# VectorE in program order in three stages of a sequence-mixing kernel, with the causal convolution's taps one pair behind its normalization

## The chip, the cores and the metric

The kernel runs on one core of one Trainium2 chip, in float32. The metric is the device time of one execution in microseconds (us). Engines are named as in the profile: PE is TensorE, DVE is VectorE, ACT is ScalarE, POOL is GpSimd and SP is SyncE, which issues most of the loads.

## What is computed

Two layers are applied one after the other to x of shape (4, 512, 128, 64): four batches, 512 time steps, and 128 frequencies of 64 channels, which together are D = 8192 columns. The change lies in the first layer, whose reference is this:

```python
xn = layernorm(x.reshape(b, t, d), ln_attn_g, ln_attn_b)
k = xn @ Wk
v = xn @ Wv
r = jax.nn.sigmoid(xn @ Wr)
decay = jnp.exp(-jnp.exp(w_decay))
# step: s = decay * s + kv_t, over time
attn = r * states @ Wo
x = x + attn.reshape(b, t, f, h)
xn = layernorm(x.reshape(b, t, d), ln_freq_g, ln_freq_b).reshape(b, t, f, h)
# convolution of 3 along the frequencies, over the 64 channels
fo = jax.nn.gelu(fo + freq_b[None, :, None])
x = x + fo
xn = layernorm(x.reshape(b, t, d), ln_time_g, ln_time_b)
# causal convolution of KS = 3 taps along time, each of the D columns by itself
to = to + time_b[None, :, None]
to = layernorm(jnp.swapaxes(to, 1, 2), time_ln_g, time_ln_b)
x = x + to.reshape(b, t, f, h)
mid = jax.nn.gelu(x @ ffn_W1 + ffn_b1)
x = x + (mid @ ffn_W2 + ffn_b2)
```

The second layer multiplies a few modes of a transform over time with learned weights, beside a moving average. It is not touched.

## The kernel before

Columns lie on the 128 partitions and the 512 time steps along the free axis. Two frequencies make a chunk of 128 columns, and two chunks make a pair, a tile of 128 by 2 by 512 (1024 elements on each partition). A batch has NPR = 32 pairs. A layernorm over all columns needs sums over the partitions and over all pairs; these are matmuls with a vector of ones (`add_up`, L249), followed by a short chain of small instructions (`finish`, `moments`, `rows`) that must end before the next stage can begin.

The first layer is cut into stages, each a Python generator that makes instructions for one pair and then yields:

- `project` (J): per pair a load of the weights, a load of x with columns on partitions, and a load of x with time on partitions ("token major"); the bn_stats of L338 on the latter (`statistics`), the scaling of the weights by the norm's gain on DVE (L355, `scale_weights`), and four matmuls of 512 columns (L407). For batch 0 there are also the matmuls of L396. For batches 2 and 3 the order of statistics and scaling is pinned and differs from that of batches 0 and 1.
- `scan` (Z): the recurrence over time, a chain of short instructions.
- `attend_and_convolve` (A): in round i, four pairs of matmuls give the attention of pair i (L527); DVE adds x (L531, into a tile `x1`, of which there are three) and scales by the rows of the norm (L535, `z`). Two rounds behind, the matmuls of the frequency convolution run (L553, L561, L569), ACT makes their gelu (L570), DVE adds `x1` (L576, `x2`), POOL stores `x2` (L577), ACT squares it (L578), and ACT scales two weight tiles for a later round (L546).
- `convolve_time` (C): per pair a load of `x2`, two DVE instructions of 1024 elements that normalize it (L625, L628, `normed`), then `tapped`: two ACT instructions that start `to` from the normalized tile (L633), four taps on DVE of 511 or 510 elements, two on each half of the tile (L637), a small correction and a store on POOL (L643, L644), and the square of `to` on ACT (L684). Its sums are added two steps behind.
- `open_feed` and `feed_forward` (O, F): residual, two matmuls with a gelu between, residual (L703 to L789).

`convolve_ahead` makes the first AHEAD = 14 pairs of the convolutions of batches 1 and 2 earlier, within the feed-forward of batches 0 and 1. For these batches `convolve_time` runs over the 18 remaining pairs, and fetches the 14 finished ones (`kh`) to square them (L691).

`in_turn` interleaves two sequences of stages. In each of eight pairs of stages it takes a step of one or of the other, according to their shares done and a lead. The pairs are:

```text
0: Z A of batch 0 | J Z of 1      4: O F of 1 | J Z of 3
1: C of 0 | A of 1                5: C of 2 | A of 3
2: O F of 0 | J Z of 2            6: O F of 2 | C O of 3
3: C of 1 | A of 2                7: F of 3 | nothing
```

The order in which instructions are made by the Python code is the program order. TensorE keeps it, by `tc.manual_schedule(engines={nc.tensor.engine})` around all of the above. For the other engines a planner chooses the order when the program is built, by its own costs; the result is a fixed sequence for each engine. Instructions given to `tc.keep_in_program_order` are exempt: they keep their place among each other. DVE, ACT and POOL each execute in the order so fixed, and wait on semaphores for what they read and for buffers to come free. The loads on SP's queue are in a fixed order as well.

Of the kernel before, what the change touches and what calls it, by code (L numbers as in the profile page):

```python
# [24 lines left out]
NPR = NCH // 2  # L25
# [55 lines left out]
def layer0(ctx, tc, dram, x, xt, vecs, wkvr, wo, wdec, wconv, fbias, w1, fb1, w2, fb2, x4):  # L81
# [4 lines left out]
    nc = tc.nc  # L86
# [18 lines left out]
    def two(pool, tag):  # L105
        return pool.tile([P, 2, SL], F32, tag=tag, name=tag)
# [183 lines left out]
    def load_x(b, i):  # L290
        xp = fr.tile([P, 2, SL], F32, tag="xp", name="xp")
        nc.sync.dma_start(xp, xt[b, 2 * i : 2 * i + 2].rearrange("c p t -> p c t"))
        return xp

    def spare(tag, n):
        return fr.tile([P, 2, n], F32, tag=tag, name=tag, bufs={"z": 4, "wx": 2}.get(tag, 3))
# [25 lines left out]
    def project(b):  # L322
        pa = two(ps_m, "m") if b == 1 else two(ps_a, "a")
        held[0] = b == 1
        if b == 0:
            psum_w = ps_p.tile([P, SL], F32, tag="p", name="psum_w")
        stt = rowp.tile([P, NT, NS, 6], F32, tag="stt", name="stt")
        def token_major(i, xk):
            s, h = i // 2, i % 2 * 2
            nc.sync.dma_start(  # L330
                xk, x[b, h * P : (h + 2) * P, s * SL : (s + 1) * SL].rearrange("(t p) d -> p t d", p=P)
            )
            return xk

        def statistics(i, xk):
            s, h = i // 2, i % 2 * 2
            for t in range(2):
                stats = nc.vector.bn_stats(stt[:, h + t, s, :], xk[:, t, :])  # L338
                if b > 1:

                    tc.keep_in_program_order(stats)

        def weights(i):

            if i < NPR:
                w = spare("wx", 4 * S + SL).rearrange("p k n -> p (k n)")[:, 0 : 16 * S]
                w = w.rearrange("p (c s) -> p c s", c=4)
                nc.sync.dma_start(w, wkvr[2 * i : 2 * i + 4, :, 0 : 4 * S].rearrange("c p s -> p c s"))
                for k in range(2):
                    ws[i + k] = w[:, 2 * k : 2 * k + 2, :]  # L350

        def scale_weights(i, wq, pinned=False):
            for j in range(2):
                w = wq[:, j, 0 : 3 * S]
                scaled = nc.vector.tensor_scalar_mul(w, w, vec[:, G1, 2 * i + j : 2 * i + j + 1])  # L355
                if pinned:
                    tc.keep_in_program_order(scaled)

        ws, xps, xks = {}, {}, {}
        if b > 1:  # L360
            weights(0)
            scale_weights(0, ws[0])
            xps[0] = load_x(b, 0)
        for i in range(NPR):
            first, last = i == 0, i == NPR - 1
            if b > 1:


                xks[i] = token_major(i, two(bk, "sq" if i % 2 else "x2"))
                if i % 2 == 0:  # L370
                    weights(i + 2)
                if not last:
                    xps[i + 1] = load_x(b, i + 1)
                wq, xp = ws.pop(i), xps.pop(i)
                for k in (i - 2, NPR - 2, NPR - 1) if last else (i - 2,):
                    if k in xks:
                        statistics(k, xks.pop(k))
            else:
                if unscanned[0]:

                    wq, xk = two(fr, "x1")[:, :, 0 : 4 * S + 3], spare("z", SL)
                else:

                    both = spare("wx", 4 * S + SL)
                    wq, xk = both[:, :, 0 : 4 * S], both[:, :, 4 * S :]
                n = 4 * S + 2 * (b == 0)
                nc.sync.dma_start(wq[:, :, 0 : n], wkvr[2 * i : 2 * i + 2, :, 0 : n].rearrange("c p s -> p c s"))
                xp = load_x(b, i)
                token_major(i, xk)
            if b == 0:  # L390
                nc.gpsimd.memset(wq[:, :, n:], 1.0)
                for j in range(2):
                    c = 2 * i + j

                    w = wq[:, j, :]
                    nc.tensor.matmul(  # L396
                        psum_w[0 : S + 2, 0 : 4 * S + 3], lhsT=w[:, 3 * S : 4 * S + 2], rhs=w,
                        start=c == 0, stop=c == NCH - 1,
                    )
            if b < 2:  # L400
                scale_weights(i, wq)
                statistics(i, xk)
            elif not last:
                scale_weights(i + 1, ws[i + 1], True)
            for j in range(2):
                for k in range(2):
                    nc.tensor.matmul(  # L407
                        pa[:, k, :], lhsT=wq[:, j, k * P : (k + 1) * P], rhs=xp[:, j, :],
                        start=first and j == 0, stop=last and j == 1,
                    )  # L410
                yield 1.0
        kvrg = rowp.tile([P, 2, SL], F32, tag="kvrg", name="kvrg")
        nc.scalar.copy(kvrg, pa)
        held[0] = False
        projected[b] = (kvrg, stt, psum_w) if b == 0 else (kvrg, stt)
# [242 lines left out]
    def convolve_time(b):  # L658
        bank = of_a if b == B - 1 else of_p
        made = AHEAD if b in ahead else 0  # L660
        moment = carried.pop(b)
        if made:
            rb, mb = ahead.pop(b)
        else:
            rb, mb = yield from rows(bank, *moment, "rm" if b == B - 1 else "rm3")
        st = bank()
        waiting, added = [], 0
        n = NPR - made
        for k in range(n + 2):
            while waiting and waiting[0][0] == k - 2:  # L670
                add_up(st, 0, *waiting.pop(0)[1:], added == 0, added == NPR - 1)
                added += 1
            if k < n:
                if b == B - 1:

                    x2, xr, to, sq = spare("xp", SL), spare("x1", SL), spare("z", SL), two(bk, "sq")
                else:
                    x2 = bk.tile([P, 2, SL], F32, tag="kx", name="x2", bufs=3)
                    xr, to = two(bk, "kd"), bk.tile([P, 2, SL], F32, tag="k3", name="to", bufs=3)
                    sq = bk.tile([P, 2, SL], F32, tag="sq4", name="sq4", bufs=2)  # L680

                normed(b, made + k, x2, xr, rb, mb, made > 0 and k < 4)
                tapped(b, made + k, xr, to)
                nc.scalar.activation(sq, to, AF.Square)  # L684
                waiting.append((k, to, sq))
                i = k * made // n
                if i != (k + 1) * made // n:

                    to = fetch("kh", tod, b, i)
                    sq = bk.tile([P, 2, SL], F32, tag="mid", name="sq5", bufs=4)  # L690
                    nc.scalar.activation(sq, to, AF.Square)  # L691
                    waiting.append((k, to, sq))
            yield 7.0 * (NPR + 2) / (n + 2)
        mean, sq = yield from finish(st, bank, 4)
        causal[b] = moments(mean, sq, 4)

# [137 lines left out]

    def in_turn(leads, *pairs):
        at, running = [0.0, 0.0], [None, None]

        def step(k):
            n = int(at[k])
            b, *stages = pairs[n][k]  # L840
            if running[k] is None:
                first = stages[0][0]
                if first in needed and b not in needed[first]:
                    return False
                running[k] = run(b, stages)
            share = next(running[k], None)
            if share == BLOCKED:
                return False
            if share is None:
                running[k] = None  # L850
                at[k] = n + 1.0
            else:
                at[k] = min(at[k] + share, n + 0.999)
            return True

        while min(at) < len(pairs):
            n = int(at[0])
            lead = leads[n] + (leads[n + 1] - leads[n]) * (at[0] - n) if n < len(pairs) else 0.0
            k = 1 if at[1] < at[0] + lead else 0
            if at[k] >= len(pairs) or not step(k):  # L860
                step(1 - k)

    def nothing(b):
        yield 1.0

    J, Z, A, C, O, F = project, scan, attend_and_convolve, convolve_time, open_feed, feed_forward
    begin[A] = 0
    needed = {A: scanned, C: carried, O: causal, F: opened}
    whole = {
        J: 2.0 * NPR, Z: 7 * CHAIN, A: 7.0 * NPR + 3 * CHAIN, C: 7.0 * (NPR + 2) + 3 * CHAIN, O: 4 * CHAIN,  # L870
# [338 lines left out]
```

## Time and profile before

| What | Value |
|---|---|
| Median of 3 runs | 3751.91 us (3749.89 to 3757.97) |
| The profiled execution | 3756.87 us |
| Its span, first to last instruction | 3755.1 us |
| Mean granted TensorE clock | 0.973 |
| TensorE busy | 3473.9 us, 93% of the span |
| DVE busy | 2675.7 us, 71% |
| ACT busy | 1778.4 us, 47% |
| POOL busy | 461.6 us, 12% |
| Moved by DMA | 910.58 MB, mean 242 GB/s |

The span runs from the first to the last instruction on the core. Busy time is the union of an engine's instructions, so two that overlap count once. A line such as L637 is a line of the kernel before. In the timeline a row gives the start, the duration from start to end, engine, line and operation, the output and the inputs with their shapes, and how many instructions are merged in it; a bracket at its end gives the time the engine stood idle before it and what it waited for. In a table of windows each row is a stretch of the span, with its length, the busy time of each engine (and instructions), the granted clock, and the share of the DMA engines that were busy.

### The profile page before, as it was taken

To read this page: it belongs to the slowest core of one execution; us is meant where nothing else is said; L and a number is where in the kernel's file an instruction comes from. 1 tells how busy PE (TensorE), PEld (TensorE's weight loads), DVE (VectorE), ACT (ScalarE), POOL (GpSimd) and SP (SyncE) were. 2 spreads that over 40 slices of the span, in tenths; PEclk is the share of its full clock that TensorE was granted. 3 is DMA by queue.
4 is the path that set the end of the run, shared out by engine and by line. 5 is a ranking of instruction groups with operands and counts; after the bars stand their busy time and mean duration, and the time that the engine had idled before them with its cause. 6 is when DMAs were issued, how large, how long until landed. Compare 5 with 4: busy or idle time off the path is not lost. (4 is left out here: it accounts for less than half of the span.)

```text
span 3755.1 us, 54524 instructions
## 1 busy us (share of the span) xinstructions
PE 3473.9 (93%) x20553; PEld 1381.1 (37%) x20553; DVE 2675.7 (71%) x3498; ACT 1778.4 (47%) x2331; POOL 461.6 (12%) x657
## 2 busy tenths in 40 slices
PE   8989988789998899999989989999988999899998
PEld 3433332224333223433322333343323843328533
DVE  4445659976767896676799699956658277792677
ACT  0013346645656564665656578868854200152100
POOL 0000013320110221011122122100000000001000
PEclk9999999999999999999999999999999999999999
DMA  9857647777885787788578577645569478894687
GB/s 309 275 197 250 227 150 265 257 265 260 291 277 169 244 285 264 269 296 273 182 252 287 202 247 267 229 157 185 201 197 283 151 240 292 287 292 165 215 284 261
DMA packets 427990, 910.58 MB, mean 242 GB/s; under 512 B 32976, under 2 KB 83920, under 8 KB 423632
## 3 DMA queue, kind: packets, MB, share of 16 engines
q1 hardware_dynamic: 354160, 637.18, 52.3%
q0 software_dynamic: 71680, 268.46, 19.9%
q8 instruction: 164, 2.69, 0.3%
q10 hardware_dynamic: 1888, 1.45, 0.1%
q14 instruction: 98, 0.80, 0.1%
HBM read 638.46 MB, written 268.50 MB: 242 GB/s over the span
## 5 line engine op out<-in xcount | busy, mean ns | idle before, releaser
L757 PE MATMUL p<-mid,w_sb 64*64 64x512 f32 x2048 | 554.1, 598 | 20.0 <-DVE wx L770 20.0
L757 PE MATMUL pb<-mid,w_sb 64*64 64x512 f32 x2048 | 535.3, 597 | 0.0
L749 ACT ACTIVATE mid<-c,fb_sb 128x1024 f32<-128x1024 f32 x256 | 284.6, 1112 | 98.7 <-PE c L744 96.5
L749 ACT ACTIVATE mid<-m,fb_sb 128x1024 f32<-128x1024 f32 x256 | 284.9, 1113 | 93.1 <-PE m L744 91.7
L744 PE MATMUL c<-x,w_sb 64*64 64x512 f32 x2016 | 281.5, 611 | 13.1 <-ACT ob L784 6.6
L744 PE MATMUL m<-x,w_sb 64*64 64x512 f32 x2016 | 282.9, 613 | 6.7 <-ACT ob L789 4.8
L757 PEld LDWEIGHTS p<-mid,w_sb 64*64 64x64 f32 x2048 | 155.5, 135 | 295.8 <-issue 262.6
L407 PE MATMUL a<-xp,wx 128*128 128x512 f32 x512 | 241.4, 615 | 9.1 <-DVE wx L355 8.6
L1055 ACT COPY two<-a 128x512 f32<-128x512 f32 x64 | 37.5, 586 | 432.9 <-PE a L1050 432.9
L1078 PE MATMUL b<-xin,avg_sb 128*128 128x512 f32 x512 | 230.8, 593 | 3.3 <-DVE xin L1084 3.3
L1084 DVE TENSOR_TENSOR xin<-b,pm 128x512 f32<-128x512 f32 x256 | 159.0, 683 | 102.9 <-PE b L1081 87.9
L527 PE MATMUL a<-rst,wo_sb 64*64 64x512 f32 x1024 | 147.8, 642 | 79.9 <-DVE x L531 78.3
L637 DVE SCALAR_TENSOR_TENSOR to<-kd,vec,to 128x510 f32<-128x510 f32 (+1 forms) x272 | 195.1, 743 | 4.2 <-issue 1.2
L712 ACT ACTIVATE kd<-kd,vec 128x512 f32<-128x512 f32 x256 | 192.9, 803 | 4.5 <-DVE kd L704 4.5
L937 DVE COPY xf<-b 128x256 f32<-128x256 f32 x128 | 54.3, 425 | 178.4 <-PE b L1024 177.4
L637 DVE SCALAR_TENSOR_TENSOR z<-x,vec,z 128x511 f32<-128x511 f32 x240 | 175.8, 744 | 5.7 <-ACT z L633 3.6
L715 DVE TENSOR_TENSOR x<-kd,kx 128x1024 f32<-128x1024 f32 x126 | 154.0, 1222 | 34.2 <-ACT kd L712 34.1
L531 DVE TENSOR_TENSOR x<-a,xp 128x1024 f32<-128x1024 f32 x128 | 156.1, 1219 | 23.0 <-PE a L527 19.3
L770 DVE SCALAR_TENSOR_TENSOR x4t<-p,fb_sb,x 128x512 f32<-128x512 f32 x64 | 47.9, 748 | 172.2 <-PE pb L757 169.8
L704 DVE TENSOR_TENSOR kd<-kd,rm 128x1024 f32<-128x1024 f32 x128 | 155.6, 1219 | 8.4 <-ACT rm L283 6.8
L703 DVE TENSOR_TENSOR kd<-kh,rm 128x1024 f32<-128x1024 f32 x128 | 155.6, 1219 | 6.0 <-ACT rm L283 3.2
L535 DVE TENSOR_TENSOR z<-x,rm 128x1024 f32<-128x1024 f32 x128 | 156.3, 1221 | 2.8
(276 smaller groups left out, 6743.2 us busy)
## 6 DMA issues: line engine op xcount, KB each, us to landing
xp<-in_xt SPq DMA_DIRECT2D x256, 512.0 KB
kh<-to SPq DMA_DIRECT2D x156, 512.0 KB
kx<-x SPq DMA_DIRECT2D x128, 512.0 KB
x<-ob POOLq DMA_DIRECT2D x64, 1024.0 KB, 8.4
xin<-x SPq DMA_DIRECT2D x64, 1024.0 KB
out<-xin POOLq DMA_DIRECT2D x64, 1024.0 KB, 6.3
x<-x POOLq DMA_DIRECT2D x98, 512.0 KB, 4.7
x<-x SPq DMA_DIRECT2D x96, 512.0 KB
```

The lines of the kernel that those rows point to most:

```text
L407: nc.tensor.matmul(pa[:, k, :], lhsT=wq[:, j, k * P : (k + 1) * P], rhs=xp[:, j, :], start=first and j == 0, stop=last and j == 1,)
L531: nc.vector.tensor_tensor(x1, at, xp, ALU.add)
L535: nc.vector.tensor_tensor(z, x1, pair_of(rb), ALU.mult)
L637: tap = nc.vector.scalar_tensor_tensor(to[:, j, k:], xr[:, j, : SL - k], vec[:, w, c], to[:, j, k:], ALU.mult, ALU.add)
L703: nc.vector.tensor_tensor(d, to, pair_of(rb), ALU.mult)
L704: nc.vector.tensor_tensor(d, d, pair_of(mb), ALU.subtract)
L712: tc.keep_in_program_order(nc.scalar.activation(d[:, j, :], d[:, j, :], AF.Identity, bias=vec[:, B4, c], scale=vec[:, G4, c]))
L744: nc.tensor.matmul(pm[halves[j], h, :], lhsT=w1_sb[halves[h], q * H : (q + 1) * H], rhs=x3[halves[h], j, :], start=True, stop=True,)
L749: nc.scalar.activation(mid, pm, AF.Gelu_apprx_tanh, bias=fb1_sb[:, q : q + 1])
L757: nc.tensor.matmul(sums2[i][j][halves[h], :], lhsT=w2_sb[halves[j], q, :], rhs=mid[halves[j], h, :], start=q == 0, stop=q == 3,)
L1078: nc.tensor.matmul(po[j], lhsT=avg_sb[:, j, :], rhs=xin[:, j, :], start=True, stop=False)
L1084: nc.vector.tensor_tensor(by_n(xin[:, j, :]), by_n(po[j]), by_c(pm[j % 2][:, j // 2, :]), ALU.add)
```

## The change

There are three edits.

1. In pairs 1, 3 and 5, those in which an `attend_and_convolve` runs beside a `convolve_time`, DVE too is put under `tc.manual_schedule`: its instructions keep the order in which the code makes them.
2. `convolve_time` normalizes pair k in step k (L625, L628) and taps pair k-1 in the same step (L633 to L644), with its square (L684) and that of any fetched `kh` (L691). There are n+3 steps instead of n+2, the sums are added three steps behind k, which is two behind the taps as before, and the weight that each step yields is adjusted.
3. `scale_weights` returns its last instruction, and in `project` for batches 0 and 1 the statistics are queued after it (`tc.issue_after`), so that L338 follows L355 of the same pair on DVE.

The built program has the same number of instructions on each engine as before: 10791 on PE, 3500 on DVE, 2347 on ACT, 662 on POOL and 1953 on SP. In the new kernel's file the lines lie a few further down: L531 becomes L532, L576 becomes L577, L637 becomes L638, and the squares of L684 and L691 move to about ten lines below.

```diff
@@ scale_weights
                 if pinned:
                     tc.keep_in_program_order(scaled)
+            return scaled.ins
@@ project
             if b < 2:
-                scale_weights(i, wq)
-                statistics(i, xk)
+                with tc.issue_after(scale_weights(i, wq)):
+                    statistics(i, xk)
@@ convolve_time
         n = NPR - made
-        for k in range(n + 2):
-            while waiting and waiting[0][0] == k - 2:
+        coming = None
+        for k in range(n + 3):
+            while waiting and waiting[0][0] == k - 3:
                 add_up(st, 0, *waiting.pop(0)[1:], added == 0, added == NPR - 1)
                 added += 1
+            tapping = coming
             if k < n:
 ...
                 normed(b, made + k, x2, xr, rb, mb, made > 0 and k < 4)
-                tapped(b, made + k, xr, to)
+                coming = xr, to, sq
+            if 0 < k <= n:
+                xr, to, sq = tapping
+                tapped(b, made + k - 1, xr, to)
                 nc.scalar.activation(sq, to, AF.Square)
-                waiting.append((k, to, sq))
-                i = k * made // n
-                if i != (k + 1) * made // n:
+                waiting.append((k - 1, to, sq))
+                for i in range((k - 1) * made // n, k * made // n):
 
                     to = fetch("kh", tod, b, i)
                     sq = bk.tile([P, 2, SL], F32, tag="mid", name="sq5", bufs=4)
                     nc.scalar.activation(sq, to, AF.Square)
-                    waiting.append((k, to, sq))
-            yield 7.0 * (NPR + 2) / (n + 2)
+                    waiting.append((k - 1, to, sq))
+            yield 7.0 * (NPR + 2) / (n + 3)
@@ in_turn
         at, running = [0.0, 0.0], [None, None]
+        region, ordered = ExitStack(), False
 ...
         while min(at) < len(pairs):
             n = int(at[0])
+            if ordered != (n in in_order):
+                ordered = not ordered
+                region.close()
+                if ordered:
+                    region.enter_context(tc.manual_schedule(engines={nc.vector.engine}))
             lead = leads[n] + (leads[n + 1] - leads[n]) * (at[0] - n) if n < len(pairs) else 0.0
             k = 1 if at[1] < at[0] + lead else 0
             if at[k] >= len(pairs) or not step(k):
                 step(1 - k)
+        region.close()
@@ the stages
     begin[A] = 0
+    in_order = (1, 3, 5)
```

## Prediction

> **What bounds the kernel now.** I read the page's head and slices first, then the windows by stage, then the timeline of VectorE (DVE) inside the stages that the change touches, and last the waits of the first stage.
>
> ```profile
> span 3755.1 us, 54524 instructions
> PE 3473.9 (93%) x20553; PEld 1381.1 (37%) x20553; DVE 2675.7 (71%) x3498; ACT 1778.4 (47%) x2331; POOL 461.6 (12%) x657
> DVE  4445659976767896676799699956658277792677
> ```
>
> Over the span TensorE is the full engine, but the DVE row has slices of 9, and these are the stages that the change puts in program order. Pair 1 (convolution of batch 0 beside attention of batch 1) runs from 545 to 803 us, pair 3 from 1242 to 1478, pair 5 from 1894 to 2140; the last two are cut where their convolution runs out.
>
> ```profile
> core 0: us, PE busy (x) PEld busy (x) DVE busy (x) ACT busy (x) POOL busy (x), PEclk, DMA share, GB/s
> 545.00:803.00 258.00, 214.85 (x1303) 64.21 (x1302) 254.47 (x278) 158.40 (x215) 81.47 (x93) 0.95 0.76 258
> 1242.00:1430.00 188.00, 169.62 (x1102) 49.43 (x1098) 181.84 (x185) 117.46 (x162) 42.87 (x61) 0.96 0.84 282
> 1430.00:1478.00 48.00, 45.95 (x298) 12.80 (x294) 22.87 (x20) 25.39 (x36) 7.25 (x10) 1.00 0.68 229
> 1894.00:2067.00 173.00, 152.97 (x990) 44.44 (x990) 169.23 (x174) 108.56 (x148) 42.66 (x57) 0.97 0.86 287
> 2067.00:2140.00 73.00, 68.01 (x441) 22.47 (x438) 46.44 (x47) 36.02 (x49) 12.01 (x17) 0.98 0.66 224
> ```
>
> In pair 1 DVE is busy 254.47 of 258 us: every DVE nanosecond added there is on the path. In pairs 3 and 5 it is full only while the convolution lasts; in the tails it is idle 25.1 and 26.6 us, and TensorE, at 45.95 of 48 and 68.01 of 73, sets the pace.
>
> What DVE pays for an instruction depends on its neighbour. In pair 1 the two stages alternate:
>
> ```profile
> 641.67 1.22 DVE L576 TENSOR_TENSOR both<-c,x 128x1024 f32<-128x1024 f32 x1
> 642.80 0.74 DVE L637 SCALAR_TENSOR_TENSOR to<-kd,vec,to 128x510 f32<-128x510 f32 x1
> 643.46 1.22 DVE L531 TENSOR_TENSOR x<-a,xp 128x1024 f32<-128x1024 f32 x1
> 644.60 0.74 DVE L637 SCALAR_TENSOR_TENSOR to<-kd,vec,to 128x511 f32<-128x511 f32 x1
> 645.26 1.21 DVE L535 TENSOR_TENSOR z<-x,rm 128x1024 f32<-128x1024 f32 x1
> ```
>
> From start to start a 1024-element instruction takes 1.13 us and a tap 0.66, less than the shown 1.22 and 0.74. In pair 3 the attention's three stand together:
>
> ```profile
> 1427.72 3.14 DVE L637 SCALAR_TENSOR_TENSOR to<-kd,vec,to 128x511 f32<-128x511 f32 x4
> 1430.97 1.22 DVE L576 TENSOR_TENSOR x<-m,x 128x1024 f32<-128x1024 f32 x1
> 1432.29 1.23 DVE L531 TENSOR_TENSOR x<-a,xp 128x1024 f32<-128x1024 f32 x1
> 1433.55 1.23 DVE L535 TENSOR_TENSOR z<-x,rm 128x1024 f32<-128x1024 f32 x1
> 1436.62 1.22 DVE L576 TENSOR_TENSOR x<-c,x 128x1024 f32<-128x1024 f32 x1 [1.85 <-ACT c L570]
> ```
>
> L576 to L531 is 1.32 us here (1.31 usually: L531 writes the x1 buffer, of three, that L576 has just read), and L531 to L535, which reads its x1, is 1.26 (1.25). The same way I read 0.779 for two taps on one half of a tile, and 1.245, once, from L625 to L628, which rewrites its output. So a dependent neighbour costs 0.175, 0.116, 0.118 and 0.11 us more.
>
> **What the Trainium skill says.** "Vector Engine (DVE) Microarchitecture Reference", section 5.2, gives 1.0417 ns a column and some 75 ns an instruction, by estimate 1.14 us for 1024; the trace agrees (1.134). "Perfetto Trace Analysis", "Optimizing Scalar/DVE Operations", says that the write-acknowledgement half of an instruction's overhead overlaps with the next; the trace agrees: 0.08 us of 1.22. "VectorE: DVE Perf Modes", "The DRAIN you can't avoid", says of eight copies that a semaphore after each costs nothing extra. Here a neighbour that waits costs 0.11 to 0.18 us; the measurement decides, but this feeds a rival.
>
> **The change part by part.** No instruction or DMA is added or removed (DVE has 3500 in both, counted in the built programs). All that changes is order, read from the built programs.
>
> *Pair 1.* Each round becomes L576, L531, L535, L625, L628 and four taps (two on one half, two on the other). Dependent neighbours rise: L576–L531 from 3 to 30, L531–L535 from 8 to 34, L625–L628 from 0 to 32, taps of one half from about 0 to 64; L637 to L625 on one kd slot falls from 7 to 3. Added: 27×0.175 = 4.7, 26×0.116 = 3.0, 32×0.11 = 3.5, 64×0.118 = 7.5, less 0.5: **+18.3 us**, 0.65 a round of 8.31. DVE is full, so nothing covers it. The edges: two L625 that now run before the first L576 follow it (+2.3); after the last L576 less is left (−3.4); the first weight scaling (L355) of the next projection now stands behind the attention's closing L266 to L275, where it used to stand ahead of that chain, and the first matmul of J2 waits some 2.4. Sum **+19.6**. Bounds +8 (L625–L628 and taps at nothing) to +24.
>
> *Pairs 3 and 5.* Eighteen convolution steps among 32 rounds. The built order puts about two behind every three attention rounds, and the last 3 rounds before the end without, against 5 before. A round with a step is 1.31 + 1.25 + 1.135 + 1.245 + 1.135 + 0.779 + 0.667 + 0.779 + 0.661 = 8.96 us. A round without is not the 3.70 of its DVE work: ScalarE, in its order, has the squares of the taps and of kh (L684, L691), that of L578, two scalings (L546) and the gelu (L570) that the next L576 needs, at pitches 0.95, 0.95, 0.95, 0.69 and 1.0; with the wait between, 4.84 from L576 to L576. Following the rounds from 1254.55 us (second L576; 1256.36 before), with TensorE's 5.65 to 7.4 us a round in the tail, the last L576 comes at 1477.2 against 1473.93: +3.3, and +2.3 for the weights behind the chain as above: **+5.6**. Pair 5 by the same count, where the next stage has no first matmul waiting longer: **+4.8**. Bounds −10 to +12 each: I multiply hand-read pitches over 30 rounds.
>
> *J0 and J1.* The statistics (L338) now follow the weight scaling. They wait on loads, and the scaling waited behind them on DVE:
>
> ```profile
> engine line waited for: us in total, times, longest us
> DVE stt L338 <- DMA z<-in_x: 53.8, 29, 8.8
> ...
> PEld a L407 <- DVE x L355: 24.6, 33, 5.5
> ...
> PE a L407 <- DVE x L355: 9.4, 7, 4.7
> ```
>
> What that can give is small, since loads are the pace: the window has a DMA share of 0.92 at 306 GB/s. TensorE needs 4.55 us for each of 31 intervals, 141.05; the weight loads are issued over 145.88; the excess is 4.8, and the first matmul comes 1.5 earlier: −6.3 at most. Against it, nine pairs' token-major loads of J1 that used to be issued early within J0 now fall into 164 to 232 us, where statistics stand ahead of the scan's short chains: +1 to +4. I take **−3** (−6.3 to +3).
>
> *Pair 6 and the rest* is not in program order; convolution of batch 3 only taps a step later, beside feed-forward work that keeps TensorE busy 269 of 300 us and hides it: 0 ± 3. The later add of statistics (L249) stands one step later in TensorE's order and costs only at a stage's end, where it is within the tails above.
>
> Sum: 19.6 + 5.6 + 4.8 − 3 + 0 = **+27.0 us**. The profiled execution took 3756.87 us, span 3755.1; it is 5 above the median of three, 3751.91, and nothing in the sum scales with that. **3779 us**.
>
> **Rivals.**
>
> *The tails close* (faster). With convolution spread to within three rounds of the end, pairs 3 and 5 could become as full as TensorE allows: busy 215.6 of 236 us and 221.0 of 246, so up to 20.4 + 25.0 = 45. At three quarters, −34 + 19.6 − 3 = −17: **3735**. It decides from 24 us recovered. For: the idle 25 us. Against: TensorE is already 96% busy in the 48 us tail, and a bare round is held at 4.84 by ScalarE.
>
> *The price is not paid.* If the 0.11 to 0.18 us come from something else than the neighbour, pair 1 keeps +1.3, pairs 3 and 5 lose some 4 each of their L625–L628 and taps, J gives −3: 1.3 + 1.6 + 0.8 − 3 = +0.7, **3753**. For: the skill's page. Against: the same lines show both pitches in one trace, by neighbour.
>
> *kh arrives late* (slower still). In pair 3 L691 waited on its load 26.5 us in 9 times, 53.0 over the run in 21, 2.5 each, behind slack. With DVE in program order a late square holds the gelu behind it, and L576 with all behind. A third of the 28 at 2.5 is 24: **3803**.
>
> That the order stays as it was is excluded by the built program.
>
> **How the numbers follow.** The sum of its parts (3765 to 3792, bounds not all at one end) 0.63; kh late 0.14; price not paid 0.10; tails close 0.13. Within 0.2%, 7.5 us, about what a measurement of this kernel can tell from no change, lies the second last and a little of the main case's fringe: 0.11. Faster 0.13, slower 0.76. The range 3748 to 3803 leaves out the closing tails and the upper part of kh late, 0.2.
>
> **What would show it.** Right: pair 1 about 277 us with as many DVE instructions; L576 to L531 at 1.31, L531 to L535 and L625 to L628 at 1.25, taps in fours of 2.96 us shown instead of twos of 1.40; the first L407 of J2 waiting on L355; rounds without a step at 4.84; J0 some 3 to 6 us shorter. Wrong: pair 1 at 258 with rounds of 8.3; DVE idle in the tails of pairs 3 and 5 much under 25 us; L691's waits well over 53 us and L576 waiting on L570 for as much.

## The result and the profile after

The changed kernel takes 3779.69 us (median of 6 runs, 3771.07 to 3789.77); the kernel before, run beside it, 3754.94 us. The ratio is 1.007, 95% interval 1.005 to 1.009: slower by 25 us. The profiled execution took 3788.66 us, 9 above the median of its kernel and 31.8 above the profiled execution of before, so the stages below show some 7 us more than the medians do.

The page's head and the DVE row of its slices, after:

```profile
span 3786.9 us, 54574 instructions
PE 3484.7 (92%) x20553; PEld 1382.8 (37%) x20553; DVE 2691.9 (71%) x3498; ACT 1783.6 (47%) x2331; POOL 435.5 (12%) x657
DVE  3445559976777886677789799956659267793677
```

DVE is busy 16.2 us longer with the same 3498 instructions. The windows after: pair 1, cut at the same places of the work as before, and pairs 3 and 5, each from the second L577 to the end of the convolution's last tap, and from there to the end of the last L577, which is the tail:

```profile
core 0: us, PE busy (x) PEld busy (x) DVE busy (x) ACT busy (x) POOL busy (x), PEclk, DMA share, GB/s
542.00:820.00 278.00, 219.99 (x1314) 62.23 (x1306) 267.82 (x278) 159.67 (x215) 64.30 (x91) 0.94 0.70 237
1270.40:1467.10 196.70, 174.61 (x1124) 50.48 (x1120) 181.19 (x181) 119.68 (x161) 41.44 (x60) 0.96 0.78 265
1467.10:1498.80 31.70, 30.43 (x202) 8.55 (x194) 14.70 (x13) 17.51 (x25) 4.46 (x7) 1.00 0.70 240
1934.20:2113.90 179.70, 157.13 (x1008) 45.12 (x1000) 170.27 (x172) 111.98 (x149) 39.42 (x57) 0.96 0.80 273
2113.90:2167.30 53.40, 51.34 (x335) 16.78 (x334) 37.62 (x36) 28.01 (x38) 7.93 (x12) 1.00 0.68 228
```

The same four stretches of pairs 3 and 5 before:

```profile
1256.40:1430.90 174.50, 159.08 (x1040) 46.22 (x1036) 168.57 (x171) 111.45 (x152) 39.72 (x56) 0.96 0.84 283
1430.90:1475.10 44.20, 42.94 (x284) 12.17 (x274) 22.00 (x18) 22.85 (x34) 5.84 (x9) 1.00 0.68 232
1908.20:2067.80 159.60, 142.44 (x932) 41.18 (x928) 156.78 (x162) 103.22 (x140) 39.75 (x53) 0.97 0.87 288
2067.80:2133.20 65.40, 63.26 (x418) 20.18 (x410) 45.02 (x42) 33.58 (x48) 9.43 (x14) 1.00 0.68 230
```

In pair 1 the same 278 DVE instructions are busy 267.82 us instead of 254.47. In pairs 3 and 5 the convolution lasts longer and the tails are shorter. In the tails DVE is idle 17.0 and 15.8 us, where it was 22.2 and 20.4; but up to the last tap it is now idle 15.5 and 9.4 us, where it was 5.9 and 2.8. The timeline of DVE in pair 1 shows a round. (Line numbers in a fence are those of the kernel that it shows. L633, L684 and L691 of before are L634, L690 and L696 in the changed kernel.)

```profile
644.35 1.22 DVE L577 TENSOR_TENSOR both<-c,x 128x1024 f32<-128x1024 f32 x1
645.66 1.23 DVE L532 TENSOR_TENSOR x<-a,xp 128x1024 f32<-128x1024 f32 x1
646.92 1.23 DVE L536 TENSOR_TENSOR z<-x,rm 128x1024 f32<-128x1024 f32 x1
648.06 1.22 DVE L626 TENSOR_TENSOR kd<-x,rm 128x1024 f32<-128x1024 f32 x1
649.32 1.23 DVE L629 TENSOR_TENSOR kd<-kd,rm 128x1024 f32<-128x1024 f32 x1
650.46 2.98 DVE L638 SCALAR_TENSOR_TENSOR to<-kd,vec,to 128x511 f32<-128x511 f32 x4
653.35 1.22 DVE L577 TENSOR_TENSOR x<-m,x 128x1024 f32<-128x1024 f32 x1
```

From L577 to L577 it is 9.00 us, with no idle time in any row: 1.31, 1.26, 1.14, 1.26, 1.14 and four taps of 2.89 together. All 24 rounds of pair 1 with one step take 9.0.

To say where time goes I cut every profiled execution at the same instructions: the first L531 of batch 1, the first L407 of batch 2, its last, the first L407 of batch 3, its last, the last L576 of batch 3, and the first matmul of the second layer. The kernels of the experiments are named below; times are us.

| Kernel | to pair 1 | pair 1 | pair 2 | pair 3 | pair 4 | pair 5 | 6 and 7 | second layer | span |
|---|---|---|---|---|---|---|---|---|---|
| before | 527.7 | 285.5 | 344.9 | 321.2 | 338.1 | 314.5 | 646.2 | 976.9 | 3755.1 |
| after | 524.5 | 307.7 | 346.4 | 326.8 | 339.5 | 321.2 | 649.0 | 971.8 | 3786.9 |
| e1 statistics alone | 526.3 | 286.9 | 346.5 | 322.3 | 340.1 | 318.3 | 646.3 | 969.4 | 3756.1 |
| e4 planner | 519.0 | 286.5 | 346.5 | 319.3 | 339.5 | 316.1 | 649.3 | 972.2 | 3748.4 |
| e2 pair 1 alone | 517.2 | 304.8 | 347.8 | 321.7 | 337.6 | 318.4 | 649.7 | 968.4 | 3765.7 |
| e3 pairs 3, 5 alone | 520.3 | 287.8 | 346.0 | 326.5 | 339.2 | 319.0 | 648.6 | 970.2 | 3757.6 |
| e5 taps in turn | 526.6 | 296.9 | 346.7 | 332.3 | 340.1 | 328.5 | 648.6 | 976.7 | 3796.5 |
| e6 interleaved | 520.5 | 286.3 | 346.9 | 337.6 | 341.5 | 330.3 | 648.9 | 970.3 | 3782.3 |
| e8 four x1 | 522.7 | 301.5 | 347.5 | 321.5 | 341.1 | 316.4 | 641.9 | 971.6 | 3764.3 |
| e7 no kh square | 518.9 | 306.3 | 347.9 | 314.6 | 341.2 | 318.3 | 650.4 | 971.7 | 3769.2 |
| e9 gelu ahead | 515.8 | 298.6 | 347.5 | 348.0 | 339.0 | 342.2 | 649.9 | 980.9 | 3821.9 |
| e10 planner, taps | 517.3 | 284.1 | 345.0 | 326.8 | 339.3 | 315.5 | 645.3 | 970.2 | 3743.5 |
| e11 and four x1 | 514.8 | 292.6 | 346.3 | 317.5 | 337.5 | 315.2 | 638.5 | 971.9 | 3734.3 |
| e12 joined | 518.4 | 285.2 | 347.5 | 319.8 | 339.3 | 315.2 | 639.9 | 974.3 | 3739.6 |

The first and the last stage show how far one execution can be trusted. After, e2 and e7 have the same order on DVE up to the end of pair 1 and still spread over 7.3 us before it; the second layer, which no edit touches, spreads over 12.5. The pairs between are steadier: pair 1 of after, e2 and e7, which share its code, is 307.7, 304.8 and 306.3. A profiled execution can lie up to 11 us from the median of its kernel (e10), so what a kernel takes as a whole is read from the ratios below, and the table only says where.

### The profile page after: what moved, and what is told of

Same layout as the page of the kernel before. It is cut to its first block, busy times and chain, and to the rows that moved or that the text cites. A ratio compares the mean times of both kernels' runs of the same rounds, so it can differ in the third digit from the quotient of the medians.

```text
span 3786.9 us, 54574 instructions
## 1 busy us (share of the span) xinstructions
PE 3484.7 (92%) x20553; PEld 1382.8 (37%) x20553; DVE 2691.9 (71%) x3498; ACT 1783.6 (47%) x2331; POOL 435.5 (12%) x657
## 5 line engine op out<-in xcount | busy, mean ns | idle before, releaser
L762 PE MATMUL p<-mid,w_sb 64*64 64x512 f32 x2048 | 562.7, 599 | 20.9 <-DVE wx L775 20.6
L749 PE MATMUL c<-x,w_sb 64*64 64x512 f32 x2016 | 286.3, 611 | 9.6 <-ACT mid L754 7.4
L528 PE MATMUL a<-rst,wo_sb 64*64 64x512 f32 x1024 | 155.7, 674 | 93.3 <-DVE x L532 91.7
L638 DVE SCALAR_TENSOR_TENSOR to<-kd,vec,to 128x511 f32<-128x511 f32 (+1 forms) x272 | 197.7, 748 | 4.8
L634 ACT ACTIVATE to<-kd,vec 128x512 f32<-128x512 f32 x136 | 103.5, 807 | 166.7 <-DVE kd L629 85.7
L532 DVE TENSOR_TENSOR x<-a,xp 128x1024 f32<-128x1024 f32 x128 | 156.7, 1224 | 34.1 <-PE a L528 25.6
L638 DVE SCALAR_TENSOR_TENSOR z<-x,vec,z 128x511 f32<-128x511 f32 x240 | 176.0, 746 | 5.6 <-ACT z L634 4.2
```

The costliest lines, as they stand in the source:

```text
L528: nc.tensor.matmul(at[hs, j, :], lhsT=wo_sb[halves[j], hs], rhs=rst[halves[j], :], start=True, stop=True)
L532: nc.vector.tensor_tensor(x1, at, xp, ALU.add)
L638: tap = nc.vector.scalar_tensor_tensor(to[:, j, k:], xr[:, j, : SL - k], vec[:, w, c], to[:, j, k:], ALU.mult, ALU.add)
L749: nc.tensor.matmul(pm[halves[j], h, :], lhsT=w1_sb[halves[h], q * H : (q + 1) * H], rhs=x3[halves[h], j, :], start=True, stop=True,)
L762: nc.tensor.matmul(sums2[i][j][halves[h], :], lhsT=w2_sb[halves[j], q, :], rhs=mid[halves[j], h, :], start=q == 0, stop=q == 3,)
```

## The experiments

Each ratio is to the kernel before, run on the same chip.

**e1, the third edit alone**, on the kernel before:

```diff
-                scale_weights(i, wq)
-                statistics(i, xk)
+                with tc.issue_after(scale_weights(i, wq)):
+                    statistics(i, xk)
```

> The kernel before with the third edit alone (in project for batches 0 and 1 the statistics follow the weight scaling on VectorE). Both theories: about 3 us faster than before, from a first projection that is some 10 us shorter (first to last L355) and a scan of batch 0 that gives most of it back. If the whole gain of the first projection stayed it would be 6 us; if nothing, 0.

3750.37 us, ratio 0.9993 (0.9982 to 1.0005): near the 3 us that were expected, but not told apart from no change. The first projection did get shorter: its last L407 started at 156.7 us instead of 163.5 (156.3 in the changed kernel).

**e4, the planner again**, on the changed kernel: `in_order = ()`.

> The changed kernel with in_order = (): the planner orders VectorE in pairs 1, 3 and 5 again, the second and third edit stay. Theory (neighbours: what costs is the 0.11 to 0.18 us that an instruction pays when its predecessor on VectorE produces or frees what it needs): the planner mixes the two stages, rounds of pair 1 are back at 8.3 us, and the whole is 20 to 28 us faster than the changed kernel, about 3752. Rival (shift: what costs is the tapping one step later, with its longer life of the kd tile and the later sums): pairs 1, 3 and 5 stay long, and the time stays near 3780.

3754.46 us, ratio 1.0002 (0.9991 to 1.0012). Pairs 1, 3 and 5 are back within 2 us of before. The shift of the taps by a step costs nothing that shows (the interval overlaps that of e1); the loss lies in program order.

**e2 and e3, program order in part**: `in_order = (1,)` and `in_order = (3, 5)`.

> The changed kernel with in_order = (1,): program order on VectorE in pair 1 alone, the planner in pairs 3 and 5. If the parts add up: from the first matmul of pair 1's attention to the first of the next projection some 21 us more than before, pairs 3 and 5 within 2 us of before, the whole 17 to 20 us slower than before, about 3772. If program order costs chiefly at the stages' edges or by what is drawn into them, pair 1 is nearer to before's.

> The changed kernel with in_order = (3, 5): the planner in pair 1, program order in pairs 3 and 5. If the parts add up: pair 1 as before within 2 us, pairs 3 and 5 some 6 us longer each, the whole 8 to 12 us slower than before, about 3763; this and the kernel with pair 1 alone together explain the changed kernel's loss.

e2: 3776.62 us, ratio 1.0052 (1.0035 to 1.007). e3: 3764.04 us, 1.0021 (1.0011 to 1.003). The parts add up: 0.52% and 0.21% make 0.73%, where the whole was 0.7%. In e2 pair 1 is 19.3 us longer than before, in e3 pairs 3 and 5 together 9.8. Both came out about as expected.

**e5, the taps in turn**, on the changed kernel, so that no tap follows the one whose result it adds to (ACT starts both halves before the first tap):

```diff
-        for j in range(2):
-            for k, w in ((1, W1), (2, W0)):
+        for k, w in ((1, W1), (2, W0)):
+            for j in range(2):
```

> The changed kernel, but the four taps of a pair go 511, 511, 510, 510 with the halves in turn, so that no tap follows the one it depends on; everything else in program order as it is. Theory (neighbours): two taps a round save 0.118 us each; pair 1 is 64 x 0.118 = 7.5 us shorter, rounds go from 9.00 to 8.77 us, pairs 3 and 5 win up to 36 x 0.118 = 4.2 us each, less what their tails hide; in all 8 to 16 us faster than the changed kernel, 3764 to 3772. Rival (fixed order: VectorE stands waiting for the one stage while the other has work ready): nothing changes, 3780.

Half of this came true. In pair 1 the rounds are 8.75 us, with 2.65 for the four taps instead of 2.89, and the pair is 296.9, 9.4 shorter than the mean of the three executions above (306.3; 7.5 expected). But pairs 3 and 5 became 5.5 and 7.3 longer than in the changed kernel, and the whole is 3789.01 us, ratio 1.0098 (1.0079 to 1.0117). Of the 15 rounds with one step in each, eight in pair 3 and six in pair 5 take 11.0 instead of 9.0. The timelines of DVE and of ACT in such a round of pair 3:

```profile
1356.26 2.73 DVE L640 SCALAR_TENSOR_TENSOR to<-kd,vec,to 128x511 f32<-128x511 f32 x4
1361.10 1.23 DVE L577 TENSOR_TENSOR x<-c,x 128x1024 f32<-128x1024 f32 x1 [2.12 <-ACT c L571]
```

```profile
1356.52 1.52 ACT L634 ACTIVATE to<-kd,vec 128x512 f32<-128x512 f32 x2 [1.83 <-DVE kd L629]
1359.10 1.06 ACT L705 ACTIVATE sq<-to 128x1024 f32<-128x1024 f32 x1 [1.06 <-DVE to L640]
1360.07 1.01 ACT L571 ACTIVATE c<-c 128x1024 f32<-128x1024 f32 x1
```

Here the planner put the square of the taps (L705) ahead of the gelu (L571) on ACT. In such a round of the changed kernel the gelu stands first: L571 starts at 1367.04 and the square, L690, at 1368.44. In e5 the square waits for the last tap, the gelu stands behind it, and DVE, whose order allows nothing else, waits 2.12 us for the gelu. DVE's waits on the gelu in pair 3 are 38.6 us in all, against 30.4 in the changed kernel and 23.8 before.

**e6, interleaved by hand**, on the changed kernel: the same three pairs in program order, but the code makes the convolution's DVE instructions between the attention's. `slots` holds two taps of the step; `fill()` makes the next one after L531 and after L576.

```diff
             nc.vector.tensor_tensor(x1, at, xp, ALU.add)
+            fill()
...
             nc.vector.tensor_tensor(x2, cv, x1s.pop(i), ALU.add)
+            fill()
...
+                one_tap(made + k - 1, xr, to, 1, 1)
+                slots.append(lambda k=k, xr=xr, to=to: one_tap(made + k - 1, xr, to, 0, 2))
+                slots.append(rest)
```

> The changed kernel, VectorE in program order in pairs 1, 3 and 5 as before, but the convolution's instructions are made between those of the attention: L576, tap, L531, tap, L535, L625, tap, L628, tap. No instruction follows the one it depends on. Theory (neighbours): rounds of pair 1 are 8.3 us instead of 9.0, pair 1 is 20 us shorter than in the changed kernel; pairs 3 and 5 win some 18 x 0.65 = 11 us less what the tails hide; in all 25 to 40 us faster than the changed kernel, 3740 to 3755. Rival (fixed order): the order is as fixed as it was, so pair 1 stays near 278 us and the whole near 3780.

Again half of it came true. DVE in pair 1:

```profile
660.08 1.22 DVE L634 TENSOR_TENSOR kd<-x,rm 128x1024 f32<-128x1024 f32 x1
661.22 0.74 DVE L666 SCALAR_TENSOR_TENSOR to<-kd,vec,to 128x511 f32<-128x511 f32 x1
661.88 1.22 DVE L639 TENSOR_TENSOR kd<-kd,rm 128x1024 f32<-128x1024 f32 x1
663.01 0.74 DVE L666 SCALAR_TENSOR_TENSOR to<-kd,vec,to 128x511 f32<-128x511 f32 x1
663.68 1.22 DVE L578 TENSOR_TENSOR x<-c,x 128x1024 f32<-128x1024 f32 x1
664.81 0.74 DVE L666 SCALAR_TENSOR_TENSOR to<-kd,vec,to 128x510 f32<-128x510 f32 x1
665.47 1.22 DVE L532 TENSOR_TENSOR x<-a,xp 128x1024 f32<-128x1024 f32 x1
666.60 0.74 DVE L666 SCALAR_TENSOR_TENSOR to<-kd,vec,to 128x510 f32<-128x510 f32 x1
667.26 1.22 DVE L537 TENSOR_TENSOR z<-x,rm 128x1024 f32<-128x1024 f32 x1
668.39 1.22 DVE L634 TENSOR_TENSOR kd<-x,rm 128x1024 f32<-128x1024 f32 x1
```

The nine instructions of a round take 8.31 us, the order as fixed as in the changed kernel, and pair 1 is 286.3, that of before. So the loss of pair 1 is the price of dependent neighbours and not of a fixed order. But pairs 3 and 5 are 10.8 and 9.1 us longer than in the changed kernel, and the whole is 3786.24, ratio 1.0089 (1.0071 to 1.0108). In pair 3, ACT and then DVE:

```profile
1369.77 1.52 ACT L660 ACTIVATE to<-kd,vec 128x512 f32<-128x512 f32 x2 [3.90 <-DVE kd L639]
1371.19 1.00 ACT L572 ACTIVATE m<-m 128x1024 f32<-128x1024 f32 x1
```

```profile
1372.22 1.22 DVE L578 TENSOR_TENSOR x<-m,x 128x1024 f32<-128x1024 f32 x1 [1.97 <-ACT m L572]
```

The start of the next taps (L660) waits for the normalization, the gelu waits behind it, and what stood between them on DVE in the changed kernel, four taps of 2.89 us, is here only one: 1.97 us idle. DVE's waits on the gelu in pair 3 are 51.8 us in all. This code also fetches the kh tiles later: their squares (L739) waited 14.4 us on the loads in pair 3, against 6.6 in the changed kernel, and no run says how much of the loss is due to that.

**e8, four x1 buffers** instead of three, on the changed kernel: `bufs=4` for the tag `x1`. L531 then writes a buffer that was read a round earlier.

> The changed kernel with four x1 buffers instead of three, all else the same: L531 (now L532) writes a buffer that was read a round earlier, and not the one that L576 ahead of it has just read. Theory (the 0.17 us from L576 to L531 are the wait for that buffer): the step from L576 to L531 falls from 1.31 to 1.14 us, rounds of pair 1 from 9.00 to 8.83, pair 1 is 26 x 0.17 = 4.4 us shorter; pairs 3 and 5 change by less than 3. Rival (it is the PSUM bank or the engine's drain that makes L531 late): 1.31 stays, and so does pair 1.

3768.0 us, ratio 1.0043 (1.0026 to 1.0059): 10 us or so of the loss are gone. DVE in pair 1:

```profile
657.33 1.22 DVE L577 TENSOR_TENSOR x<-c,x 128x1024 f32<-128x1024 f32 x1
658.46 1.22 DVE L532 TENSOR_TENSOR x<-a,xp 128x1024 f32<-128x1024 f32 x1
659.71 1.22 DVE L536 TENSOR_TENSOR z<-x,rm 128x1024 f32<-128x1024 f32 x1
```

From L577 to L532 it is 1.13, from L532 to L536 still 1.25: the wait was for the buffer, and only that one went. Rounds are 8.81 us, pair 1 is 301.5, 4.8 below the mean. More than expected came elsewhere. Pairs 3 and 5 are 5.3 and 4.8 shorter than in the changed kernel; in each of them L577 to L532 fell 28 times from 1.31 to 1.135, which is 4.9 us. So the price of this neighbour counts in full there too. Pairs 6 and 7 are shorter by 7.1. The convolution of batch 3 takes x1 tiles too; its last L625 started 279.8 us after the last L576 in the changed kernel and 269.0 here. In the three kernels with four x1 buffers (e8, e11, e12) this is 266.8 to 269.0, in all others 276.3 to 281.5.

**e7, without the kh squares**, on the changed kernel:

```diff
-                    sq = bk.tile([P, 2, SL], F32, tag="mid", name="sq5", bufs=4)
-                    nc.scalar.activation(sq, to, AF.Square)
-                    waiting.append((k - 1, to, sq))
+                    waiting.append((k - 1, to, to))
```

> The changed kernel without the squares of the fetched kh tiles on ScalarE (L691 of before); the second moment of the convolutions of batches 1 and 2 is then summed from the kh tiles themselves, so the output is not the reference's. Theory (ScalarE's order sets when the gelu comes, and a fixed VectorE waits for it): the rounds of pairs 3 and 5 without a convolution step lose 0.95 us and the wait for the load, down to 3.7 us at least; VectorE's waits on the gelu in pair 3, 30.4 us, fall to about 20, and pair 3 is 5 to 9 us shorter, pair 5 3 to 6. Rival (those rounds are held by TensorE): rounds and both pairs stay within 2 us.

3772.7 us, ratio 1.0044 (1.0028 to 1.006). In the changed kernel a round of pair 3 without a step ran so, ACT first and then DVE:

```profile
1355.62 1.06 ACT L696 ACTIVATE sq<-kh 128x1024 f32<-128x1024 f32 x1 [1.24 <-DMA kh<-to]
1356.58 1.04 ACT L579 ACTIVATE both<-both 128x1024 f32<-128x1024 f32 x1
1357.53 0.78 ACT L547 ACTIVATE wcs<-wc_sb,vec 128x192 f32<-128x192 f32 x2
1358.22 1.00 ACT L571 ACTIVATE m<-m 128x1024 f32<-128x1024 f32 x1
```

```profile
1359.25 1.23 DVE L577 TENSOR_TENSOR x<-m,x 128x1024 f32<-128x1024 f32 x1 [2.31 <-ACT m L571]
```

Without L696 DVE's waits on the gelu in pair 3 fell from 30.4 us to 16.6, and pair 3 from 326.8 to 314.6 (12.2 shorter, 5 to 9 expected), pair 5 by 2.9. The two lists of waits, of after and of e7:

```profile
DVE x L577 <- ACT m L571: 13.3, 5, 3.6
DVE x L577 <- ACT c L571: 11.4, 6, 3.6
DVE both L577 <- ACT c L571: 3.6, 1, 3.6
DVE both L577 <- ACT m L571: 2.1, 1, 2.1
```

```profile
DVE x L577 <- ACT m L571: 6.9, 2, 3.6
DVE x L577 <- ACT c L571: 4.0, 2, 3.6
DVE both L577 <- ACT c L571: 3.6, 1, 3.6
DVE both L577 <- ACT m L571: 2.1, 1, 2.1
```

What is left stands behind the last tap, all but 0.4 us, and the eight rounds without a step that lie between those with one take 3.7 to 3.9 us, where they took 3.7 to 7.2. So in pair 3 what ACT does ahead of the gelu is on the path. The run takes away the square and the wait for its load at once, and doesn't say how much is each.

**e9, the gelu ahead**, on e6: ACT in program order too, the gelu first in a round, squares behind it, the taps' start a round ahead. For that the attention's sums and its convolution's matmuls moved ahead of the step of the convolution in TensorE's order.

```diff
+            if b and i > 3:
+                if i < NPR + 2:
+                    head(i - 2)
+                yield 7.0
+                if i < NPR + 2:
+                    tail(i - 2)
...
-                    region.enter_context(tc.manual_schedule(engines={nc.vector.engine}))
+                    region.enter_context(tc.manual_schedule(engines={nc.vector.engine, nc.scalar.engine}))
```

> VectorE and ScalarE both in program order in pairs 1, 3 and 5, with the convolution's VectorE instructions between those of the attention (no instruction behind the one it depends on), and on ScalarE the gelu first in each round, the squares of the convolution behind it, and the start of the taps a round ahead, so that nothing that waits for a late instruction stands ahead of the gelu. Theory (in pairs 3 and 5 the fixed VectorE loses by waiting for a gelu that ScalarE has behind other work): waits for the gelu fall below 10 us a pair, rounds are 8.3 us with and 3.7 to 4.8 us without a step, pair 1 is as long as before, pairs 3 and 5 some 8 us shorter each than before, the whole about 3735. Rival (the waits come from TensorE or from loads): pairs 3 and 5 no shorter than before, 3755 or more.

The expectation failed: 3824.8 us, ratio 1.0179 (1.0158 to 1.0201). Rounds without a step take 7.8 us, and DVE's waits on the gelu in pair 3 are 56.7 us, where less than 10 were expected. Pair 1 is 12.3 longer than in e6. The gelu is no longer late behind ACT's own work but behind TensorE; from ACT's waits in pair 3:

```profile
ACT c L576 <- PE c L575: 46.1, 15, 5.4
ACT m L576 <- PE m L575: 45.5, 15, 5.4
```

So the rival, that the waits come from TensorE, holds for this order. TensorE is busy nine tenths of these pairs, and its matmuls were moved to suit ACT. The run changes both orders at once; what ACT's order alone would give was not measured.

**e10 and e11, the planner with taps in turn**: e1, and the taps 511, 511, 510, 510, kept so with `tc.keep_in_program_order` for batches 1 and 2; e11 has four x1 buffers besides.

> The kernel before with the third edit, the planner on VectorE throughout, and the taps 511, 511, 510, 510 with the halves in turn (pinned among themselves for batches 1 and 2). A candidate for a version better than both. Theory (in pairs 3 and 5 the planner's order still has two dependent taps in most steps, fours of 3.13 us): up to 18 x 0.24 = 4 us shorter in pair 3 and in pair 5, pair 1 the same, the whole 5 to 10 us faster than before, about 3747. Rival (a late gelu takes up what the taps give, as it did with both orders fixed): no faster than the third edit alone, 3751 or slower.

> The same with four x1 buffers. Theory: where L531 follows L576 in pairs 3 and 5, some 25 times each, 0.17 us less, 2 to 4 us a pair as far as VectorE sets the pace there; the whole about 3743. Rival (gelu or TensorE set the pace): as the kernel without the fourth buffer, within 3 us.

e10: 3756.55 us, ratio 1.0004 (0.9992 to 1.0017), where 5 to 10 us were expected: nothing gained. Pair 3 is 5.6 us longer than before. DVE now waited 8.1 us there for the start of a tile's second half, which the second tap of four now needs; but e11 has 7.2 us of the same wait and a shorter pair 3, so what made it longer stays open. e11: 3745.85 us, ratio 0.9982 (0.9973 to 0.999), faster, though pair 1 is 7.1 longer than before, with 15.4 us of waits on the gelu. Its profiled execution is 10 us under its median, and ahead of pair 1 that can be chance; pairs 6 and 7, 7.7 us shorter than before, agree with e8.

**e12, joined**: e11, with pair 1 as in e6.

> A candidate that joins what the runs favour: the third edit; four x1 buffers; in pair 1 alone VectorE in program order, with the convolution's instructions between those of the attention so that none follows the one it depends on; in pairs 3 and 5 the planner, with the taps 511, 511, 510, 510. Theory: pair 1 takes 286 us (292.6 in the kernel with four x1 buffers under the planner alone, where VectorE waited 15 us on the gelu), pairs 3 and 5 about 317 and 315, the whole 6 us faster than that kernel, about 3740, 14 below before. Rival (the fixed order costs as much at its waits as it saves by its neighbours): pair 1 at 292 or more, the whole 3746 or more.

3744.82 us, ratio 0.9972 (0.9963 to 0.9982): faster than before by 10 us, where 14 were expected, and than the changed kernel by some 35. It is not told apart from e11, whose interval overlaps. Pair 1 takes 285.2, as expected, which is also what it took before. By the stages its gain over before is chiefly pairs 6 and 7 (6.3, four x1 buffers) and the stretch ahead of pair 1 (9.3 in this execution, of which e1, by its ratio, answers for 2.6, and the rest is within what that stretch varies by).

## Why the prediction was right

The forecast was 3779, the measured median 3779.69. That the two agree within 1 us is luck: the change was forecast as 27.0 us on top of a median of 3751.91, and it measured 24.75 on top of 3754.94. The step that carried the forecast was read from before's trace and held: a dependent neighbour on DVE has a price, and program order puts dependent instructions side by side. For pair 1 this is shown by runs. For pairs 3 and 5 the totals came out near the forecast, but not by its working.

- **Pair 1**: forecast 8.96 us a round and +19.6 in all. Measured 9.00, and +19.3 to +22.2 in the three executions of this code. The trace has 28, 28, 32 and 64 more of the four dependent neighbours, where I counted 27, 26, 32 and 64. The 0.04 us by which a round is longer than forecast lie half in independent neighbours (1.142 instead of 1.135, and 0.667 instead of 0.661 from the last tap to L577), half in L532 to L536 and L626 to L629 (1.259 and 1.255 instead of 1.25 and 1.245). The terms, taken away one by one: L576 to L531 forecast 4.7 (e8: 4.8), the taps 7.5 (e5: 9.4), everything 18.3 (e6: 20.0). Each is a difference to the mean of three executions that spread over 2.9 us. The rival that the price isn't paid is out.
- **First matmul of the next projection behind L355**: forecast 2.4 later after pair 1 and 2.3 after pair 3. From the last L576 to the first L407 it was 5.43 us before both, and 7.78 and 7.74 after.
- **Pair 3**: forecast +5.6, measured +5.5 before rounding, but by two errors that cancel. The second L576 came, counted from the last L407 of pair 2, 6.4 us earlier than before, where I had 1.8; and from there to the last L576 it took 227.2 us, where I had 222.7. The rounds with a step were 9.0 as forecast. Eight rounds without one between them took 3.7 to 7.2, in the mean 5.1, against 4.84 for all. Why the second L576 came so early stays open.
- **Pair 5**: forecast +4.8, measured +6.8 before rounding. **Pair 6 and the rest**: forecast 0 ± 3, measured +2.8.
- **J0 and J1**: forecast −3, measured −3.2 ahead of pair 1 and −2.6 by e1's ratio, though its interval holds 0, and the stretch ahead of pair 1 varies by more. The first projection itself won 7.2, a little beyond the 6.3 that I gave as the most; in all 13 kernels with the third edit its last L407 starts at 155.4 to 159.9 us instead of 163.5. The waits show the queue dissolved: L338's 53.8 us are gone from the list, and L355 waits for TensorE instead, as the waits on the first 157 us say:

```profile
DVE x L355 <- PE psum_w L397: 77.2, 30, 4.8
...
PEld a L408 <- DVE x L355: 17.5, 32, 3.7
```

- **kh late**: out as a late load, since L691 waited 16.1 us on its load over the whole run instead of 53.0. The other half of that rival, a square that holds the gelu and L576 behind it, is what e7 shows for pair 3.
- **The tails close**: out as a gain. The tails lost 5.2 and 4.6 us of idle time on DVE, where 24 had to come back, and up to the last tap DVE became idle 9.6 and 6.6 us more. In pair 3 up to there its waits on the gelu went from 2.4 us to 13.8.

Not foreseen was how much in pairs 3 and 5 depends on what a fixed DVE waits for. The price is paid there too, as e8 shows. But e5 and e6 removed dependent neighbours and lost time: in their timelines the planner's order on ACT leaves the gelu late, and DVE has nothing else that it is allowed to take. That the gelu's place on ACT is the cause is shown by a run only for the kh squares (e7); for e5 and e6 it is argued from the timelines and the summed waits.

## What to carry to other kernels

Where an engine is full, the start-to-start time of each pair of neighbours is worth reading from the trace: mixing two independent streams instruction by instruction hides waits that program order, one stream's block after the other's, exposes, even with the instructions unchanged. A fixed order on one engine makes it depend on the order that a planner chose for the others, so a saving there can come back as a wait; fixing it is safest in a stage where that engine is full. Here even that (e12) is not told apart from leaving the planner its order (e11). A buffer more can be worth more than an order: it removed one of the waits here, and a stage that used the same buffers ended sooner.

## What the runs showed of the hardware

Two VectorE instructions in a row, of which the second needs the first to be finished, cost 0.11 to 0.18 us more than two independent ones: 1.26 against 1.14 us where the second reads the first's output, 1.31 where it overwrites a buffer that the first reads, 0.78 against 0.66 for taps on one half of a tile. A fourth buffer took the 1.31 to 1.13 (e8). One independent instruction in between took the cost away: the nine instructions of a round are 8.31 us in e6 and 9.00 in the changed kernel. "VectorE: DVE Perf Modes" of the Trainium skill, section "The DRAIN you can't avoid", says of eight copies in a row that a semaphore after each costs nothing extra. Here, in float32 and with about 512 or 1024 elements on each partition, a neighbour that has to wait does cost something, and the measurement decides.
